# Text attention scored once in 32x32 array tiles, with each partition's own maximum and in-place transposes on VectorE, in three of four batches

## Chip, cores and metric

The kernel runs on one core of one Trainium2 chip. The metric is the device time of one execution in microseconds. Five engines have queues of their own: PE (TensorE, matmuls), DVE (VectorE), ACT (ScalarE), POOL (GpSimd) and SP (here only DMA issues). Each takes its instructions strictly in the order of the program; they meet through semaphores.

## The reference

A layer with cross attention and a quantised feed-forward part, on 4 batches of 1024 tokens with 512 channels. Of the 1024 tokens, 768 are "image" tokens in three chunks of 256, which attend to their own chunk; the last 256 are "text" tokens, which attend to all image tokens and causally to the text tokens. 16 heads of 32 channels.

```python
def trinity_mask(txt_tok, img_tok):
    sit = img_tok // 3
    img_img = (i < img_tok) & (j < img_tok) & (i // sit == j // sit)
    txt_img = (i >= img_tok) & (j < img_tok)
    txt_txt = (i >= img_tok) & (j >= img_tok) & (i >= j)
    return img_img | txt_img | txt_txt

def xattn(q, kv, ...):          # B, N, C = 4, 1024, 512; H = 16; d = 32
    qh, kh, vh = heads(q @ Wq + bq), heads(kv @ Wk + bk), heads(kv @ Wv + bv)
    scores = jnp.einsum('bhqd,bhkd->bhqk', qh, kh) * d ** -0.5
    attn = softmax(where(mask, scores, -inf), axis=-1)
    out = jnp.einsum('bhqk,bhkd->bhqd', attn, vh)
    return out.transpose(0, 2, 1, 3).reshape(B, N, C) @ Wo + bo

x = x + xattn(layernorm(x), ctx, ...)
x = x + ffn(layernorm(x), ...)   # gate, up (512 -> 1408), silu, down; int8-like fake quantisation
```

## The kernel before

The program has an attention stage (to about 874 us of the profiled execution) and a feed-forward stage behind it. All instructions of PE, DVE, ACT and POOL stand in an order that the program writes out by hand (`manual_schedule`, L819).

**Blocks and units.** A block is 256 query tokens of one batch (`Block`, L412). A unit (`Unit`, L424) is one block with one group of four heads (`g`, 128 channels); in a text block also one of four parts of 256 keys, so that a text block has 16 units and an image block 4. The batches come in turn: three image blocks and the text block; in the last batch the text block comes second. There are 112 units.

**The loop over units** (L864) makes one step per unit, and each step works on several units at once: scores of unit n, transposed scores and exponentials of unit n-5 (`T_LAG`), values of unit n-6 (`V_LAG`). Between them stands one "large" piece: a quarter of a key/value projection, a half of a query projection (`big_step`), or half of an output projection (`step_output`); `large` and `target` say which, by a count of work. Each is about 3.4 us of PE.

**Scores are made twice.** `maxima` (L435) makes scores with queries on partitions, four heads in four row groups of the array (32 x 128 tiles, L446 for image, L457 for text), and DVE takes the row maximum (L450, L468; in text the causal mask is added first, L467). POOL splits the negated maximum into two bfloat16 parts (`minus_maxima`, L472), and a DMA transpose brings them into a row (`shifts`, L488). `weights` (L495) makes the scores a second time with keys on partitions (L509), on top of a matmul that lays the shift into the same PSUM tile (L504); ACT takes two exponentials of 1024 columns (L514, L518). POOL adds the weights up over the key tiles (L535). `values` (L539) multiplies the values with the weights in four column groups (128 x 32 tiles, L554), and the sums with ones (L573); ACT copies both out, DVE takes the reciprocal (L588) and POOL the product (L589), which is the normalised output with channels on partitions.

**Projections.** `load_spread` (L142) loads a block of tokens so that one DVE transpose of 32x32 blocks (L267) turns it; its source is read with a step of four elements, since channel 4p + k goes with row p of weight slice k. PSUM: three pairs of two banks for scores (`ps_sc`), one bank for values (`ps_av`), one for projections (`ps_mm`).

**Weights of the feed-forward part** are quantised in the attention stage: per 128 rows a load, a maximum on DVE, a quantisation on ACT and POOL, and a DMA transpose into `wgT` and `wuT`, which stay on chip (`weight_unit`, L645).

Of the kernel before, what the change touches and what calls it, by code (L numbers as in the profile page):

```python
# [42 lines left out]
def kernel(ctx: ExitStack, tc: tile.TileContext, x, kv, Wq, bq, Wk, bk, Wv, bv, Wo, bo, clip_x, clip_down, w_gate, w_up, w_down, out):  # L43
# [39 lines left out]
    wgT = cpool.tile([P, NCC, FF], BF16, tag="wgT", name="wgT")  # L83
    wuT = cpool.tile([P, NCC, FF], BF16, tag="wuT", name="wuT")
# [36 lines left out]

    with ExitStack() as actx:
# [3 lines left out]
        qp = actx.enter_context(tc.tile_pool(name="qp", bufs=4))  # L126
        kp = actx.enter_context(tc.tile_pool(name="kp", bufs=7))
        ap = actx.enter_context(tc.tile_pool(name="ap", bufs=1))
        wp = actx.enter_context(tc.tile_pool(name="wp", bufs=1))
# [12 lines left out]
        def load_spread(src, c):  # L142
            t = ld.tile([P, NQB * 2, P], F32, tag="cb", name=f"spread_{c}")
            s = src.rearrange("(k q) (c m) -> c q k m", q=D, c=NCC)
            for i in range(NCC):
                nc.sync.dma_start(t[i * D : (i + 1) * D], s[i])
            return t

# [13 lines left out]
        for _ in range(14):  # L162
            nc.tensor.matmul(idle.rearrange("p (a b) -> p a b", a=4), onesb, rhs, start=True, stop=True)
        cb0 = load_block(kv_tok, 0, "cb")
        for ci in range(NCC):
            (nc.sync if ci % 2 == 0 else nc.scalar).dma_start(W["Wk"][:, ci, :], Wk.rearrange("(p k) f -> k p f", k=NCC)[ci])
# [4 lines left out]
        for name, w in (("Wv", Wv), ("Wq", Wq)):  # L171
            nc.sync.dma_start(W[name], w.rearrange("(p k) f -> p k f", k=NCC))
# [15 lines left out]
        def output_bias():  # L188

            bvr = wk2.tile([P, NCC, D], F32, tag="wst", name="bvr", bufs=1)  # L190
            parts = wk2.tile([P, C], F32, tag="sp", name="bo_parts")
# [24 lines left out]


        Q, K, V = {}, {}, {}
# [17 lines left out]
        def prepare(a):  # L236

            j = jobs[a]
            if j.kind == "kv":
                spreads[a] = load_spread(kv_tok[j.c * QB : (j.c + 1) * QB, :], f"kv_{j.c}")  # L240
                return
            spreads[a] = load_spread(xn_d[j.c], f"q_{j.c}")
            next_queries(j.c)
# [7 lines left out]
        class Job:  # L251
# [8 lines left out]
            def run_small(self):  # L260
# [4 lines left out]
                if self.c > 0:  # L265
                    src = spreads.pop(self.a)
                    nc.vector.transpose(self.T.rearrange("p c (k q) -> p k c q", q=D), src.rearrange("p k (e c) -> p k c e", c=NCC))  # L267
                    return
# [6 lines left out]
                cols = src[:, i, :].rearrange("p (f k) -> p k f", k=NCC)  # L275
                for cc in range(NCC):
                    nc.tensor.transpose(pt[:, cc, :], cols[:, cc, :], ident)
# [24 lines left out]
            def first_rows(self):  # L302

                K[0] = kp.tile([P, NCC, QB], F32, tag="kT", name="kT_0")
# [14 lines left out]
            def run_big(self, half=False):  # L319
# [8 lines left out]
                elif i < 2:  # L328
                    if i == 0 and first:
                        K[c] = kp.tile([P, NCC, QB], F32, tag="kT", name=f"kT_{c}")  # L330
                    rest = self.rows(K[c], "Wk", NCC, 1.0, 2 * i, parts)
                else:
                    i -= 2
                    if i == 0 and first:
                        V[c] = kp.tile([P, 2, C], F32, tag="va", name=f"va_{c}")
# [16 lines left out]
        background = deque()  # L352
        ready = {}

        def normalise(c):
# [25 lines left out]
            def apply():  # L381
                for i in range(2):
                    nc.scalar.activation(xb[:, i, :], xb[:, i, :], AF.Identity, bias=t[:, i : i + 1], scale=s[:, i : i + 1])
                if c > 0:
                    nc.sync.dma_start(xn_d[c].rearrange("(t p) c -> p t c", p=P), xb)
                ready[c] = True
# [23 lines left out]
        OUTS = 3  # L410
# [13 lines left out]
        class Unit:  # L424
            def __init__(self, block, g, part, parts):
                self.k, self.g, self.part, self.parts = block, g, part, parts
                self.direct = False
                self.n = f"{block.n}_{g}_{part}"
# [6 lines left out]
        def maxima(u):  # L435
# [15 lines left out]
            else:  # L451
# [12 lines left out]
                for h in range(2):  # L464
# [3 lines left out]
                    nc.vector.tensor_reduce(nmh[:, h, :, i, half], s[:, :, :n], AX.X, ALU.max, negate=True)  # L468

# [25 lines left out]
        def weights(u, between):  # L495
# [16 lines left out]
            pT = wk2.tile([P, 4, 2, QB], F32, tag="pT", name=f"pT_{u.n}")  # L512
# [26 lines left out]
        def values(u, between, more=False):  # L539
# [7 lines left out]
            av = state["av"]  # L547
            diag = k.text and u.part == TEXT
# [15 lines left out]
            if last:  # L564
# [19 lines left out]
                avs = small.tile([P, 2, QB], F32, tag="avs", name=f"avs_{u.n}", bufs=2)  # L584
# [58 lines left out]
        quantised = [False]  # L643

        def weight_unit(n):  # L645

            src, dst, scales, what = (w_gate, wgT, sg, "g") if n % 2 == 0 else (w_up, wuT, su, "u")
# [3 lines left out]
            w8 = wk2.tile([P, C], I8, tag="w8", name=f"w8_{what}_{ic}", bufs=1)  # L651
            q = wk2.tile([P, C], BF16, tag="wqt", name=f"wq_{what}_{ic}", bufs=1)
# [9 lines left out]
            def quantise():  # L662
                nc.scalar.activation(w8, w, AF.Identity, scale=rcp)
                nc.gpsimd.tensor_copy(q, w8)
                quantised[0] = True

            def transpose():
                nc.sync.dma_start_transpose(dst[:, :, ic * P : (ic + 1) * P], q)

            return largest, quantise, transpose  # L670

        T_LAG, V_LAG = 5, 6
        units = []
        for b in range(B):
            for qb in range(NQB) if b < B - 1 else (0, TEXT, 1, 2):
                k = Block(b, qb)
                parts = NQB if k.text else 1
                units += [Unit(k, g, part, parts) for g in range(NCC) for part in range(parts)]
        n_img, n_text = NCC * TEXT, NCC * NQB
# [3 lines left out]
        for i, u in enumerate(units):  # L683
            u.direct = u.direct or u.part == TEXT and i + V_LAG >= LATE
        last_of = {c: max(n for n, u in enumerate(units) if c in u.k.keys) for c in range(NC_)}


        then_q = dict(zip(Q_ORDER, Q_ORDER[1:] + [None]))
# [3 lines left out]
        KV_BUFS = 7  # L692
# [3 lines left out]
        def prepare_next(n, force=False):  # L696

            a = at_small
            if a < len(jobs) and a > 1 and a not in prepared:
                j = jobs[a]  # L700
                while force and j.kind == "q" and not ready.get(j.c):
                    background.popleft()()
# [573 lines left out]
```

## Time and profile before

| what | us |
|---|---|
| three runs | 1127.98, 1126.76, 1128.59 (median 1127.98) |
| span of the profiled execution | 1126.9 |
| first scores of a unit start | 30.7 |
| the three text blocks of batches 0, 1, 2 | 128 to 252, 342 to 465, 554 to 676 |
| last output projection of the attention stage starts | 873.7 |
| first matmul of the gate starts, last one | 884.1, 1038.4 |
| mean granted TensorE clock | 0.995 |

Times on the page are microseconds from the span's start unless they are marked ns. A line of a group names the source line, the engine, the operation, the tile written and the tiles read, the shapes and the number; then busy time and mean ns of one; then the idle time of the engine just before them and what ended most of it. A float32 matmul leaves two MATMUL records. Matmuls overlap each other, so the mean ns of one is longer than what each adds to the busy time.

### The profile page before, as it was taken

What the parts mean: (1) busy time and instruction counts of PE and PEld (TensorE: products, weight loads), DVE (VectorE), ACT (ScalarE), POOL (GpSimd) and SP (SyncE); (2) the same over time, 40 slices, a digit from 0 to 9 for tenths busy, and PEclk for the clock granted to TensorE, in tenths of its full rate; (3) what the DMA queues carried; (4) which work ended last, traced back from release to release, by engine and by line L of the source; (5) the groups of instructions that cost most, each with busy time, mean ns of one, the idle gap of its engine ahead of it and who ended that gap; (6) DMA issues with size and microseconds to landing.
All of it is one profiled execution on the core that took longest, in us unless ns stands there. A gap on an engine that the chain in (4) does not pass through costs nothing.

```text
span 1126.9 us, 31493 instructions
## 1 busy us (share of the span) xinstructions
PE 1106.6 (98%) x13829; PEld 553.9 (49%) x13851; DVE 783.9 (70%) x980; ACT 502.4 (45%) x701; POOL 532.0 (47%) x615
## 2 busy tenths in 40 slices
PE   9999999999999999999999999999999899998998
PEld 5545545454545444454545445555554344443344
DVE  2546677666576857666777657777667788877887
ACT  3234434353544334444434345545433465553553
POOL 1224546577755467775446467566752222110110
PEclk9999999999999999999999999999999899999999
DMA  7379645255744444332222113112321599310895
GB/s 234 101 219 284 114 96 127 61 113 98 121 62 115 93 105 78 101 81 63 59 84 80 48 60 83 47 51 63 114 67 58 179 295 255 70 38 23 302 386 194
DMA packets 138257, 135.87 MB, mean 121 GB/s; under 512 B 56060, under 2 KB 103432, under 8 KB 136712
## 3 DMA queue, kind: packets, MB, share of 16 engines
q1 hardware_dynamic: 115600, 91.91, 29.5%
q0 software_dynamic: 22208, 41.42, 14.3%
q8 instruction: 108, 1.77, 0.7%
q10 hardware_dynamic: 312, 0.53, 0.2%
q14 instruction: 29, 0.24, 0.1%
HBM read 79.96 MB, written 50.07 MB: 115 GB/s over the span
## 4 chain that ended last, share of the span: by engine, by line
PE 87%; POOL 4%; DVE 3%; ACT 2%; DMA 2%; issue 1%; SPq 0%; DVEq 0%; POOLq 0%; ACTq 0%
PE pv L226 10%; PE po L226 9%; PE av L554 9%; PE pp_q L226 8%; PE pp_kv L226 8%; PE t L509 7%; PE pg L1116 7%; PE pu L1116 7%; PE s L457 5%; PE pd L1219 5%; PE s L446 4%; POOL sp L535 3%; PE av L573 3%; PE t L504 3%; PE pd L1207 1%
## 5 line engine op out<-in xcount | busy, mean ns | idle before, releaser
L514 ACT ACTIVATE pT<-t 128x1024 f32<-128x1024 f32 x112 | 114.8, 1025 | 330.2 <-PE t L509 299.8
L535 POOL TENSOR_TENSOR sp<-sp,pT 128x1024 f32<-128x1024 f32 x84 | 189.3, 2254 | 43.2 <-ACT pT L518 39.8
L468 DVE TENSOR_REDUCE nmh<-s 128x2 f32<-128x1024 f32 (+1 forms) x128 | 145.2, 1157 | 61.2 <-PE s L457 59.0
L535 POOL TENSOR_TENSOR sp<-pT 128x1024 f32<-128x1024 f32 x59 | 140.2, 2375 | 95.7 <-ACT pT L518 87.3
L450 DVE TENSOR_REDUCE nmh<-s 128x4 f32<-128x1024 f32 x96 | 112.7, 1216 | 85.7 <-PE s L446 85.7
L226 PE MATMUL pp_q<-qT,Wq_sb 128*32 128x256 f32 x2048 | 121.3, 380 | 0.2
L226 PE MATMUL pv<-Wv_sb,kvT 128*32 128x512 f32 (+1 forms) x1088 | 120.5, 570 | 0.0
L554 PE MATMUL av<-pT,va 128*32 128x256 f32 (+1 forms) x1792 | 116.9, 377 | 0.0
L518 ACT ACTIVATE pT<-t 128x1024 f32<-128x1024 f32 x112 | 114.5, 1023 | 0.0
L509 PE MATMUL t<-qT,kT 32*128 32x256 f32 (+1 forms) x1792 | 113.8, 367 | 0.0
L226 PE MATMUL pp_kv<-kvT,Wk_sb 128*32 128x256 f32 x1920 | 112.5, 380 | 0.1
L226 PE MATMUL po<-Wo_sb,oT 128*32 128x512 f32 (+1 forms) x1120 | 112.1, 534 | 0.3
L588 DVE RECIPROCAL avs<-avs 128x256 f32<-128x256 f32 x63 | 109.8, 1743 | 0.0
L589 POOL TENSOR_TENSOR oT<-avs 128x256 f32<-128x256 f32 x63 | 48.0, 762 | 104.2 <-DVE avs L588 104.2
L509 PEld LDWEIGHTS t<-qT,kT 32*128 32x128 f32 x1792 | 88.3, 184 | 6.6
L1116 PE MATMUL pg<-xqT,wgT 128*128 128x512 bf16 x344 | 89.9, 381 | 1.1 <-DVE xqT L1077 0.5
L1116 PE MATMUL pu<-xqT,wuT 128*128 128x512 bf16 x345 | 89.8, 381 | 0.4
L1122 ACT ACTIVATE silu<-pg,sg 128x512 f32<-128x512 f32 x88 | 60.0, 686 | 64.9 <-PE pg L1116 62.8
L226 PEld LDWEIGHTS pp_q<-qT,Wq_sb 128*32 128x32 f32 x2048 | 63.3, 110 | 48.3 <-issue 5.8
L1143 DVE SCALAR_TENSOR_TENSOR h<-pu,su,silu 128x512 f32<-128x512 f32 x88 | 65.3, 746 | 30.3 <-PE pu L1116 27.6
L226 PEld LDWEIGHTS pp_kv<-kvT,Wk_sb 128*32 128x32 f32 x1920 | 60.2, 110 | 43.6 <-issue 2.3
L554 PEld LDWEIGHTS av<-pT,va 128*32 128x32 f32 x1792 | 47.0, 109 | 53.5 <-issue 30.3
(190 smaller groups left out, 1435.0 us busy)
## 6 DMA issues: line engine op xcount, KB each, us to landing
xt<-x_d SPq DMA_DIRECT2D x16, 1024.0 KB, 6.0
h<-h_d POOLq DMA_DIRECT2D x3, 2816.0 KB, 13.5
xb<-in_x_dram SPq DMA_DIRECT2D x16, 512.0 KB, 4.4
x_d<-bo_b SPq DMA_DIRECT2D x16, 512.0 KB, 5.7
x_d<-in_x_dram POOLq DMA_DIRECT2D x16, 512.0 KB, 7.6
xr<-x_d SPq DMA_DIRECT2D x16, 512.0 KB, 3.8
x_d<-xr POOLq DMA_DIRECT2D x16, 512.0 KB, 3.8
spread_kv<-in_ctx_dram SPq DMA_DIRECT2D x60, 128.0 KB, 3.0
```

Source lines behind the costliest of these rows:

```text
L226: nc.tensor.matmul(out[rows_of(j)], lhs[:, rows_of(j)], rhs, start=start, stop=stop, tile_position=(0, j * D), skip_group_check=True)
L450: nc.vector.tensor_reduce(nmh[:, h, :, :, 0], prs[h], AX.X, ALU.max, negate=True)
L468: nc.vector.tensor_reduce(nmh[:, h, :, i, half], s[:, :, :n], AX.X, ALU.max, negate=True)
L509: nc.tensor.matmul(prs[j // 2][:, j % 2, n, cols], kc[rows_of(j), g, n * P : (n + 1) * P], q[rows_of(j), g, cols], start=False, stop=(n == 1))
L514: nc.scalar.activation(pT[:, :2], prs[0], AF.Exp)
L518: nc.scalar.activation(pT[:, 2:], prs[1], AF.Exp)
L535: nc.gpsimd.tensor_tensor(sp[:, :, cols], a, pT[:, :, n, cols], ALU.add)
L554: nc.tensor.matmul(av[rows_of(j), 0, cols], va[:, n, g * P + j * D : g * P + (j + 1) * D], u.pT[:, j, n, cols], start=(u.part == 0 and n = ...
L588: nc.vector.reciprocal(avs[:, 1, :], avs[:, 1, :])
L1116: nc.tensor.matmul(ps, w[:, cc, ic * P : (ic + 1) * P], qT[:, cc, :], start=(cc == 0), stop=(cc == NCC - 1))
L1122: nc.scalar.activation(s, pg, AF.Silu, scale=sg[:, ic : ic + 1])
L1143: nc.vector.scalar_tensor_tensor(h[:, ic, :], pu, su[:, ic : ic + 1], s, ALU.mult, ALU.mult)
```

## The change

In batches 0, 1 and 2 a text unit is now 64 consecutive queries (two blocks of 32) against all the keys they may attend to, for four heads; there are still 16 of them per text block (`u.rows`). The text block of batch 3 and all image blocks keep the old way.

- `block_scores` makes scores once, in 32 matmuls of 32 x 32 array tiles: 4 heads on the row groups, 4 key sets on the column groups, 2 query blocks. A partition then holds one query and a quarter of its keys. DVE adds a mask to the last 16 columns and takes the partition's own maximum (`own`).
- `exponents`: eight exponentials (one per head and query block, 208 to 256 columns, bias is the own maximum), each with a sum of its row (`accum_out`).
- `spread_out`, `exchange`, `differences`, `factors`, `inverses`: the four partitions that hold one query get each other's maxima and sums through a matmul with a 0/1 matrix (`same`), and from them one factor per row.
- `scaled`: POOL multiplies the exponentials in place by the factor, so that they are normalised. `turned`: DVE transposes them in place in 32x32 blocks, after which keys lie on partitions.
- `row_values`: one product with the values for each two units, in four column groups, 28 or 32 matmuls per half block of queries; ACT copies the result straight to `oT`.

Beside it: five empty steps (`GAP`) ahead of each of these text blocks; projections in these blocks are counted 1.2 to 1 (`TEXT_PACE`); keys of a batch in one tile, two of them (`kp`), six value and three query buffers; `pT`, `avs` and the new exponentials share three buffers (`bp`); the contraction order of the projections is changed so that the transposes of L267 read consecutive elements, and weights are loaded in pieces to match; text keys of batches 0 to 2 are loaded with every fourth token together (`turned=True`); the quantised gate and up weights are transposed into a small tile, written to DRAM and loaded back when the projection weights are no longer needed (`reload`); stores and weight transposes are issued one step later (`posts`).

The core of the diff:

```diff
+        def block_scores(u):
+            k, g, q, keys = u.k, u.g, Q[u.k.c], KB[u.k.b]
+            u.s = prs = [pair(f"s_{u.n}_{h}") for h in range(2)]
+            u.own = small.tile([P, 2, 8], F32, tag="own", name=f"own_{u.n}", bufs=3)
+            for a in range(2):
+                block = slice((2 * u.part + a) * D, (2 * u.part + a + 1) * D)
+                for x in range(4):
+                    for j in range(4):
+                        nc.tensor.matmul(
+                            prs[j // 2][x * D : (x + 1) * D, j % 2, a, :].rearrange("p (k n q) -> p k n q", n=2, q=D),
+                            q[rows_of(j), g, block],
+                            keys[rows_of(j), g].rearrange("p k (n g q) -> p g k n q", n=2, q=D)[:, x],
+                            start=True, stop=True, tile_position=(j * D, x * D), skip_group_check=True,
+                        )
+            u.width = 3 * 2 * D + 16 * (u.part + 1)
+            for h in range(2):
+                s, w = prs[h], u.width
+                nc.vector.tensor_tensor(s[:, :, :, w - 16 : w], s[:, :, :, w - 16 : w], mask16..., ALU.add)
+                nc.vector.tensor_reduce(out, s[:, :, :, :w], AX.X, ALU.max, negate=True)
+        def exponents(u, h):
...
+            for x in range(4):
+                y = 4 * h + x
+                nc.scalar.activation(
+                    u.e[:, y // 2, 2 * (u.part % 2) + y % 2, :w], u.s[h][:, x // 2, x % 2, :w], AF.Exp, bias=u.own[:, 0, y : y + 1], accum_out=u.own[:, 1, y : y + 1]
+                )
+        def spread_out(u):
+            nc.gpsimd.tensor_tensor(u.ex, own, group.unsqueeze(2).to_broadcast([P, 4, 16]), ALU.mult)
+        def exchange(u):
+            bank_ = ps_av.tile([P, 2, QB], F32, tag="av", name=f"all_{u.n}")
+            nc.tensor.matmul(bank_[:, 0, :64], same, u.ex.rearrange("p x c -> p (x c)"), start=True, stop=True)
+        def differences(u):
+            nc.vector.tensor_reduce(least, u.all[:, :, 0, :].rearrange("p x y -> p y x"), AX.X, ALU.min)
+            nc.vector.tensor_tensor(u.w[:, :4], least.unsqueeze(1).to_broadcast([P, 4, 8]), u.all[:, :, 0, :], ALU.subtract)
+            nc.vector.tensor_tensor(u.w[:, 4], least, u.own[:, 0, :], ALU.subtract)
+            nc.vector.tensor_copy(u.sums, u.all[:, :, 1, :])
+        def factors(u):
+            nc.gpsimd.tensor_tensor(u.w[:, :4], u.w[:, :4], u.sums, ALU.mult)
+            nc.gpsimd.tensor_tensor(u.w[:, :2], u.w[:, :2], u.w[:, 2:4], ALU.add)
+            nc.gpsimd.tensor_tensor(u.w[:, 0], u.w[:, 0], u.w[:, 1], ALU.add)
+        def inverses(u):
+            nc.vector.reciprocal(u.w[:, 0], u.w[:, 0])
+        def scaled(u):
+            nc.gpsimd.tensor_tensor(u.f, u.w[:, 4], u.w[:, 0], ALU.mult)
...
+            if u.part % 2 == 0:
+                nc.gpsimd.memset(half[:, :, :, u.width : u.width + 16], 0.0)
+            for h in range(2):
+                e = half[:, 2 * h : 2 * h + 2, :, : u.width]
+                nc.gpsimd.tensor_tensor(e, e, f, ALU.mult)
+        def turned(u):
+            w = 7 * D if u.part < 2 else QB
+            for h in range(2):
+                e = u.e[:, 2 * h : 2 * h + 2, 2 * (u.part % 2) : 2 * (u.part % 2) + 2, :w]
+                nc.vector.transpose(e, e)
+        def row_values(u):
+            av = ps_av.tile([P, 2, QB], F32, tag="av", name=f"av_{u.n}")[:, 0, :]
+            half, blocks = u.part // 2, 7 if u.part < 2 else 8
+            for x in range(blocks):
+                for j in range(4):
+                    nc.tensor.matmul(
+                        av[rows_of(j), :P].rearrange("p (a q) -> p a q", q=D),
+                        V[k.keys[x // 2]][:, x % 2, g * P + j * D : g * P + (j + 1) * D],
+                        u.e[:, j, :, x * D : (x + 1) * D],
+                        start=(x == 0), stop=(x == blocks - 1), tile_position=(0, j * D), skip_group_check=True,
+                    )
+            nc.scalar.copy(k.oT[:, g, half * P : (half + 1) * P], av[:, :P])
```

The order of one step in the loop, with `now` the unit of this step, `r1` and `r2` those one and two steps back, and `r` three back (`R_LAG`):

```diff
+            if r is not None and r.part % 2:
+                row_values(r)
...
+                if u.rows and u.k.text:
+                    block_scores(u)
+                else:
+                    maxima(u)
...
+            if r1 is not None:
+                spread_out(r1)
...
+            if now is not None:
+                exponents(now, 0)
             full = large(n)
+            if now is not None or r1 is not None:
+                complete()
+            if r1 is not None:
+                exchange(r1)
+                differences(r1)
+            if now is not None:
+                exponents(now, 1)
+            if r1 is not None:
+                nc.scalar.activation(r1.w, r1.w, AF.Exp)
+                factors(r1)
+            if r2 is not None:
+                turned(r2)
+            if r1 is not None:
+                inverses(r1)
+                scaled(r1)
```

## The prediction

> **What bounds the kernel now.** I read the busy totals first, then the chain of work that ended last, then that chain in order of time in one text block, then the costliest groups, and last a table of busy time by stretch.
>
> ```profile
> PE 1106.6 (98%) x13829; PEld 553.9 (49%) x13851; DVE 783.9 (70%) x980; ACT 502.4 (45%) x701; POOL 532.0 (47%) x615
> ...
> PE 87%; POOL 4%; DVE 3%; ACT 2%; DMA 2%; issue 1%; SPq 0%; DVEq 0%; POOLq 0%; ACTq 0%
> ```
>
> TensorE is busy for 98% of the span and carries 87% of the chain that ended last; no other engine has a twentieth of it. One step (one unit's scores to the next unit's) in a text block, from that chain in order of time; the columns are start, length, engine, tile, line and number of records (a float32 matmul leaves two):
>
> ```profile
> 151.99 3.57 PE po L226 x32
> 155.56 0.33 PE t L504 x4
> 155.88 0.86 PE t L509 x16
> 156.75 1.00 PE av L554 x16
> 157.75 0.43 PE av L573 x8
> 158.18 3.43 PE pv L226 x32
> 161.61 1.08 PE s L457 x16
> ```
>
> The pieces touch: nothing but TensorE sets the pace. The table by stretch says the same for a whole text block of 16 steps, with the other engines at 43 to 70%:
>
> ```profile
> core 0: us, PE busy (x) PEld busy (x) DVE busy (x) ACT busy (x) POOL busy (x), PEclk, DMA share, GB/s
> 128.00:252.00 124.00, 122.75 (x1832) 61.87 (x1832) 86.76 (x108) 52.95 (x80) 76.24 (x74) 1.00 0.44 96
> 342.00:465.00 123.00, 122.55 (x1836) 61.71 (x1832) 88.68 (x112) 51.82 (x77) 72.50 (x67) 1.00 0.45 100
> ```
>
> So a text step takes 123/16 = 7.7 us, and the other engines have 2.3 to 4.4 us of it free. The groups from which the new operations are priced, with mean ns and idle time:
>
> ```profile
> L535 POOL TENSOR_TENSOR sp<-sp,pT 128x1024 f32<-128x1024 f32 x74 | 176.6, 2386 | 42.4 <-ACT pT L518 39.8
> L589 POOL TENSOR_TENSOR oT<-avs 128x256 f32<-128x256 f32 x63 | 48.0, 762 | 104.2 <-DVE avs L588 104.2
> L267 DVE STREAM_TRANSPOSE qT<-spread_q 128x1024 f32<-128x1024 f32 x15 | 32.0, 2132 | 26.3 <-PE pp_q L226 15.9 <-DMA spread_q<-xn_d 8.0 <-PE pv L226 2.3
> L450 DVE TENSOR_REDUCE nmh<-s 128x4 f32<-128x1024 f32 x96 | 112.7, 1216 | 85.7 <-PE s L446 85.7
> L309 PE MATMUL pk<-kvT,Wk_sb 128*128 128x256 f32 x32 | 7.2, 382 | 0.1
> L226 PE MATMUL pp_q<-qT,Wq_sb 128*32 128x256 f32 x2048 | 121.3, 380 | 0.2
> ```
>
> The last two show what array tiles give: the same 256 columns cost 7.2/32 = 225 ns on the whole array and 121.3/2048 = 59 ns in four column groups at once.
>
> **The change on TensorE alone.** Out, for one head group of a text block (four units): scores 1.08, shift product 0.33, transposed scores 0.86, values 1.00, four times each, and the sums 0.43: 13.5 us. In: four times 32 score matmuls, 64 records of 256 columns in 32x32 tiles. No row has sixteen tiles at once. If all sixteen run together they are four waves of 216 ns, 0.86 us; at the 59 ns of four groups they are 3.8 us. I take 0.86, since these tiles are row groups (L509, 16 records in 0.86) crossed with column groups (L226), and each kind alone reaches nearly fourfold. With 0.2 for the change of array shape (1.08 against 0.86 above), 4.2 us. Four exchange matmuls of 64 columns, 0.3 each with its change of shape: 1.2. Values: 60 matmuls with 128 columns, 120 records at half of 1.00/16: 3.7. Sum 9.1, so 4.4 us saved; times 12 groups (three batches), 53 us. If TensorE stayed the bound: 1126.9 - 53 = 1074 us, and 18 us less for a text block: 105 us.
>
> [...]
>
> **The change on the other engines, by step.** ScalarE: eight exponentials with a bias and a sum in place of two of 1024; 256 columns with a bias take 471 ns (L295), two follow each other in 0.84, so 3.4 us, and reading eight sums costs from nothing to 8 x 0.2 (the shortest ScalarE rows, L371). With one projection's eviction (0.9), the exponential of the differences and the copy of the values, 5 to 6.7 us. VectorE: two masks 0.5, two maxima over some 930 columns 2.2, four small operations on 8 to 32 columns 0.7 (L478: 169 ns), a reciprocal 0.2, two transposes. These have no dense row. L267 takes 2.13 us for 1024 but reads with a step of four elements; the new ones read in order, as does L450, 1.2 us. For 960 on average that is 1.1 or 2.0 each. I take 1.1, since the order of reading is what sets L267 apart; 2.0 goes into the range. In all 5.8 or 7.6, and 0.9 of spreading and statistics.
>
> [...]
>
> GpSimd: in place of the running sums (2.39 per 1024, seven in four units) two in-place products over 930 columns. It is the same operation, L535: 2.39 x 930/1024 = 2.17 each, 4.35; spreading 64 elements 0.35 (between L485, 8 elements, 239 ns, and L589), three factors 0.7, one scale and half a memset 0.35. 5.8 us.
>
> Every engine's sum is under 7.7 us. But they are not independent, and this is the step that decides. In the new order GpSimd issues the spreading of unit k+1 behind the products of unit k; TensorE's exchange of k+1 waits for the spreading; VectorE's differences of k+1 wait for the exchange; behind them in VectorE's queue stand the transposes of k, and behind these the reciprocal of k+1; GpSimd's products of k+1 wait for the reciprocal. That is a loop through three engines that is run once for each unit:
>
> - spreading 0.35
> - exchange, VectorE waiting on it, 0.5 (the lone matmul pair L112 keeps VectorE idle 0.6 with 128 columns)
> - differences 0.7
> - transposes of the unit before 2.2 (ScalarE's exponential and GpSimd's factors, 1.1, beside them)
> - reciprocal 0.2, scale and memset 0.35, some 0.15 for hand-overs
> - products 4.35
>
> 8.8 us, against TensorE's 105/16 = 6.6. No projection can be moved into the hole by the hardware, as TensorE takes its instructions in order and the next projection stands behind the exchange. The engines' other work (maxima 2.7 us, exponentials) fits beside the 4.35 of the products. A text block then takes 27 + 15 x 8.8 = 159 us: an estimated 23 until the first unit's products end (two steps of TensorE and one pass of the loop), and 4 for the last unit's transposes and values. That is 54 us more than 105, 162 for three blocks: 1074 + 162 = **1236 us**, and this is the forecast. The loop becomes harmless at 27 + 15 x P = 105 + 18, P = 6.4 us, where the 53 us saved are just used up.
>
> Edits costed at nothing, as TensorE's queue covers them: the projections' transposes now read in order (one micro-second off, or none, thirty times, off the path; the chain shows L267 once); the quantised gate and up weights go to DRAM and come back in two loads, 1.4 MB each (h<-h_d, 2.8 MB, lands in 13.5 us), issued on SP's queue while the last image blocks run; uncovered, they would hold the feed-forward stage up by some 14 us. The stores and transposes of weights wait on SP's queue behind compute once more per piece; the loads behind them have several steps to spare. Weight rows loaded in pieces of 2 KB: bounds -3 to +3 us at the start (Wk lands in 5 to 6 now). The five empty steps ahead of a text block hold their projections and the image units' remains, so their work only moves. Fewer key and query buffers: the order on TensorE already has it.
>
> **Rivals.**
> 1. Transposes stay at 2.0 each. For it: the only row of a transpose. Against: its reading step. The loop is 10.6, a block 186, 1074 + 243 = 1317 us.
> 2. The loop is shorter, not slower than before: GpSimd's product with a repeated factor runs at the pace of one input. L1067 (512 elements, 622 ns) and L1099 (1408, 1362) give 0.83 ns an element, 0.97 each, so P = 6.4, the 27 becomes 25, a block 121 and the time 1122 us; with the hand-overs overlapped, 6.25, 1115. It decides from about 1 us a product. Against: L535 and L589 are this very operation at 2.3 and 3.0 ns an element.
> 3. Sixteen tiles do not run together: 3.8 in place of 0.86 us. In the steps where the loop has room (6.6 + 2.9 against 8.8) it costs 0.7, and in the first three of a block 2.9: 3 x (13 x 0.7 + 3 x 2.9) = 53 more, 1290 us. Against: the two kinds of groups each run together.
> 4. The loop is hidden and TensorE bounds: 1074 us. For it: TensorE is the bound now. Against: the order of the queues.
>
> **Numbers.** The forecast 0.58, rival 1 0.18, rival 3 0.09, rival 2 0.08, rival 4 0.03, others 0.04. The range 1140 to 1335 leaves out rivals 2 and 4, some of rival 1 above it, and the others. The forecast's own range, from products of 2.0 to 2.4 and waits that add up to half a microsecond a step, is 1205 to 1275. This kernel's runs lie within 0.16% of each other, so 0.2% is about what can be told from no change. Faster: most of rival 2, and rival 4, 0.08; within 0.2%: 0.02; slower: 0.90. The profiled execution took 1126.9 us and the median of the runs is 1127.98, so I add 1: 1237.
>
> **What would show it.** In a text block TensorE busy near 70%, idle before the exchange matmul and released by GpSimd; VectorE's idle before the small minimum released by that matmul; GpSimd's idle before the scale released by the reciprocal. A score unit of 0.9 to 1.1 us, a transpose near 1.1, a product near 2.2, steps of 8.8 us. I am wrong if the products take 1 us, if text steps are below 6.5 us, or if the time goes to the feed-forward stage, which should keep its 249 us from the first L112 (878) to the end.

## The result, and the profile after

The changed kernel takes 1371.5 us (median of four runs, 1371.4 to 1371.9) where the kernel before takes 1128.3 beside it: a ratio of 1.216, 95% interval 1.214 to 1.217, so slower by 243 us. The forecast was 1237 us with a range to 1335. The direction was right; the time lies 134 us above the forecast and above the range.

The page of the profiled execution (span 1369.7 us, mean granted clock 0.911 where it had been 0.995) begins with the busy totals; then the slices of the span, and the chain of work that ended last by engine:

```profile
PE 1170.8 (85%) x15915; PEld 592.4 (43%) x15915; DVE 872.2 (64%) x1341; ACT 588.3 (43%) x1434; POOL 549.0 (40%) x845
...
PE   9899977675899877757998877558999989999898
...
PEclk9999998886899988877999888669999999999999
...
PE 70%; DVE 12%; POOL 8%; ACT 5%; issue 3%; DMA 1%; SPq 0%; DVEq 0%; POOLq 0%
```

TensorE is no longer the only engine of the chain, its share of the span falls from 98 to 85%, and in the three places where it is least busy the granted clock falls too. That TensorE's busy time rises from 1106.6 to 1170.8 is the surprise: the forecast had it fall by 53.

The table by stretch, for the first text block (from its first scores to the first image scores), the image units and empty steps after it, and two neighbouring pieces within the block, cut where the clock changes; behind it the image stretch of the kernel before:

```profile
core 0: us, PE busy (x) PEld busy (x) DVE busy (x) ACT busy (x) POOL busy (x), PEclk, DMA share, GB/s
162.40:332.80 170.40, 127.16 (x2396) 67.00 (x2393) 108.74 (x217) 81.67 (x320) 86.12 (x144) 0.84 0.35 79
332.80:448.90 116.10, 104.40 (x1444) 51.26 (x1446) 73.82 (x92) 40.54 (x62) 59.33 (x80) 0.94 0.51 97
286.40:293.20 6.80, 5.35 (x109) 3.79 (x120) 3.11 (x7) 3.18 (x12) 4.12 (x8) 0.50 0.63 81
293.20:306.90 13.70, 9.88 (x227) 5.36 (x196) 11.07 (x25) 6.51 (x28) 7.27 (x16) 1.00 0.19 53
```

```profile
252.00:342.00 90.00, 88.14 (x1296) 43.26 (x1288) 56.61 (x59) 39.13 (x57) 64.61 (x78) 1.00 0.57 94
```

A text block takes 170.4, 167.2 and 165.6 us (159 forecast). Its steps are not even: after the first four they alternate between some 5.5 and 14 to 15 us, some 20.2 for a pair of units. The last two rows of the first table together last about as long as such a pair: 6.8 us at half clock, 13.7 at full.

The trace's clock records hold two values only, 1.0 and 0.5. That allows the loss to be added up, for the time to the gate's first matmul, as a sum over TensorE's records. "Half clock" is half of the time that TensorE was busy while the clock was 0.5. It is an estimate of what the low clock added, since it takes all work to last twice as long there; in this trace eight records of an output projection took 1.93 us at half clock and 1.04 at full, 64 score records 2.38 and 1.49.

| us | before | after | difference | forecast |
|---|---|---|---|---|
| TensorE's work at full clock | 872 | 857 | -15 | -53 |
| added by half clock | 1 | 78 | +76 | no term |
| TensorE idle | 10 | 191 | +180 | +162 |
| gate starts | 884.1 | 1125.8 | +242 | +109 |

After that little differs: 249.7 us from the first L111 to the end, against 248.6 from the first L112 before, as forecast.

Where the time lies is another matter. The three text blocks take 503 us against 369, 134 more (forecast 108). The stretches around them, up to the gate, take 108 more, where the forecast had nothing: 116.1 in place of 90.0 in the rows above, for one. Some work went over: TensorE's work at full clock falls by 57 us within the text blocks, and some 24 us of that (by the number of their records) are projections that now stand outside; outside, work rises by 42. Of the 191 us idle 133 lie within the text blocks and 58 outside, of the 78 by half clock 61 and 17.

The groups whose prices the forecast had to guess (busy, mean ns; idle before them and its releaser), with shapes kept apart:

```profile
L592 POOL TENSOR_TENSOR E<-E,fac 128x1024 f32<-128x1024 f32 x24 | 44.9, 1894 | 0.9
L592 POOL TENSOR_TENSOR E<-E,fac 128x832 f32<-128x832 f32 x24 | 37.3, 1574 | 0.0
L599 DVE STREAM_TRANSPOSE E<-E 128x1024 f32<-128x1024 f32 x48 | 57.0, 1221 | 2.0 <-POOL E L592 1.8
L599 DVE STREAM_TRANSPOSE E<-E 128x896 f32<-128x896 f32 x48 | 50.3, 1085 | 0.0
```

and, where the shape does not matter:

```profile
L546 ACT ACTIVATION_READ_ACCUMULATOR E<-s,own 128x1 f32 x384 | 83.1, 216 | 0.0
L521 PE MATMUL s<-kT,qT 32*32 32x256 f32 x3072 | 81.2, 436 | 2.6 <-ACT E L546 2.6
L608 PE MATMUL av<-E,va 128*32 128x128 f32 x1440 | 96.6, 418 | 65.6 <-DVE E L599 65.6
L559 PE MATMUL all<-ex,same 128*128 128x64 f32 x96 | 23.2, 327 | 74.4 <-POOL ex L554 74.4
```

The transposes cost 1.1 to 1.2 us, as forecast; the products 1.6 to 1.9, less than the 2.17 forecast. The small score tiles, 81.2 us busy for 3072 records, are 26 ns each (64 records: 1.7 us, or 1.49 where the clock was full; forecast 0.86 and 0.2), and the values products 67 ns (forecast 31). TensorE waits in the two places that are new in its queue: for the spreading (L554) ahead of the exchange, and for the transposes (L599) ahead of the values product. So far this looks like the forecast's loop. The chain in order of time (start, length, engine, tile, line, records) shows another; one pair of steps:

```profile
248.98 3.20 PE av L608 x52
252.18 1.48 PE s L521 x60
253.66 3.64 PE pp_kv L260 x64
...
257.32 0.84 ACT kT L330 x2
258.16 1.67 ACT E L546 x8
259.83 0.13 ACT wall L1120
...
260.03 0.26 POOL wall L574
...
260.90 0.21 DVE wall L580
...
261.46 3.75 POOL E L592 x2
265.21 0.26 POOL ex L554
...
265.52 0.45 PE all L559 x2
...
265.99 0.20 DVE least L567
...
266.58 0.31 DVE E L599
...
267.66 1.21 DVE E L599
...
268.91 3.63 PE av L608 x60
```

From one values product to the next, 19.9 us, the chain passes through four engines' queues in turn: values product, next scores, a projection; then ScalarE, which must evict that projection and finish the unit's exponentials before it comes to the exponential of the differences; factors, reciprocal, one pair of GpSimd products; spreading, exchange, differences, transposes; and the values product again. It is run once for two units. The forecast's loop, with the measured prices, would be 0.27 + 0.5 + 0.6 + 2.1 + 0.2 + 0.35 + 0.15 + 3.5 = 7.7 us a unit, shorter than the 10.1 that a unit takes.

### The profile page after: what moved, and what is told of

Its sections match the earlier page's. It is cut to its first block, busy times and chain, and to the rows that moved or that the text cites. A ratio compares the mean times of both kernels' runs of the same rounds, so it can differ in the third digit from the quotient of the medians.

```text
span 1369.7 us, 37140 instructions
## 1 busy us (share of the span) xinstructions
PE 1170.8 (85%) x15915; PEld 592.4 (43%) x15915; DVE 872.2 (64%) x1341; ACT 588.3 (43%) x1434; POOL 549.0 (40%) x845
## 4 chain that ended last, share of the span: by engine, by line
PE 70%; DVE 12%; POOL 8%; ACT 5%; issue 3%; DMA 1%; SPq 0%; DVEq 0%; POOLq 0%
PE pv L260 7%; PE po L260 7%; PE pp_q L260 7%; PE av L608 6%; PE pp_kv L260 6%; PE pg L1352 6%; PE pu L1352 6%; POOL E L592 5%; PE av L708 4%; PE pd L1455 4%; DVE E L599 4%; PE t L660 4%; PE s L488 3%; PE s L521 3%; ACT E L546 3%
## 5 line engine op out<-in xcount | busy, mean ns | idle before, releaser
L546 ACT ACTIVATE E<-s,own 128x208 f32<-128x208 f32 (+3 forms) x384 | 169.6, 465 | 154.0 <-DVE own L535 138.4
L592 POOL TENSOR_TENSOR E<-E,fac 128x832 f32<-128x832 f32 (+3 forms) x96 | 164.4, 1734 | 1.9
L687 POOL TENSOR_TENSOR sp<-pT 128x1024 f32<-128x1024 f32 x47 | 111.7, 2376 | 119.1 <-ACT pT L670 92.0
L608 PE MATMUL av<-E,va 128*32 128x128 f32 x1440 | 96.6, 418 | 65.6 <-DVE E L599 65.6
L666 ACT ACTIVATE pT<-t 128x1024 f32<-128x1024 f32 x64 | 65.6, 1024 | 169.3 <-PE t L660 162.8
L535 DVE TENSOR_REDUCE own<-s 128x4 f32<-128x832 f32 (+3 forms) x96 | 108.0, 1125 | 3.3
L599 DVE STREAM_TRANSPOSE E<-E 128x896 f32<-128x896 f32 (+1 forms) x96 | 107.3, 1153 | 2.0 <-POOL E L592 1.8
L608 PEld LDWEIGHTS av<-E,va 128*32 128x32 f32 x1440 | 70.5, 169 | 86.7 <-issue 60.3
L742 DVE RECIPROCAL pT<-pT 128x256 f32<-128x256 f32 x51 | 88.9, 1743 | 20.3 <-ACT pT L1182 20.3
L559 PE MATMUL all<-ex,same 128*128 128x64 f32 x96 | 23.2, 327 | 74.4 <-POOL ex L554 74.4
L521 PE MATMUL s<-kT,qT 32*32 32x256 f32 x3072 | 81.2, 436 | 2.6 <-ACT E L546 2.6
```

The lines of the kernel that those rows point to most:

```text
L521: nc.tensor.matmul(prs[j // 2][x * D : (x + 1) * D, j % 2, a, :].rearrange("p (k n q) -> p k n q", n=2, q=D), q[rows_of(j), g, block], key ...
L535: nc.vector.tensor_reduce(out, s[:, :, :, :w], AX.X, ALU.max, negate=True)
L546: nc.scalar.activation(u.e[:, y // 2, 2 * (u.part % 2) + y % 2, :w], u.s[h][:, x // 2, x % 2, :w], AF.Exp, bias=u.own[:, 0, y : y + 1], ac ...
L592: nc.gpsimd.tensor_tensor(e, e, f, ALU.mult)
L599: nc.vector.transpose(e, e)
L608: nc.tensor.matmul(av[rows_of(j), :P].rearrange("p (a q) -> p a q", q=D), V[k.keys[x // 2]][:, x % 2, g * P + j * D : g * P + (j + 1) * D] ...
```

## The experiments

Twelve kernels, each timed in one round against the kernel before; intervals are given with the ratios. Theory G is the forecast's loop, theory A the loop of the chain above, T that TensorE itself is the bound, K that the halved clock is a cause and not only a symptom.

**late**: the values product goes from the front of its step to its end.

```diff
-            if r is not None and r.part % 2:
...
-                row_values(r)
...
             if r1 is not None:
                 inverses(r1)
                 scaled(r1)
+            if r is not None and r.part % 2:
...
+                row_values(r)
```

> The values product (row_values) is moved from the front of its step to its end, behind the exchange. Theory A (a loop over two units: values product 3.6, scores 1.5, projection 3.6, its eviction 0.8 and the exponentials 1.7 on ScalarE, then factors, GpSimd products, exchange, differences, transposes 2.0, and again the values product, 20.3 us a pair): the loop falls apart, what is left is the forecast's loop with measured prices, 7.6 us a unit, so a text block goes from 167 to some 130 us and the whole to 1240 to 1290 us. Theory G (the forecast's loop through spreading, exchange, transposes, reciprocal and products already sets the pace and the values product waits beside it): no more than 10 us less, 1360 us. Theory T (TensorE's lower clock and slow small tiles set the pace): within 15 us of 1371.

Measured 1311.3 us, 1.164 (1.161 to 1.167): 60 us less. Theory T falls, and G too, since its loop was not touched. But A expected 80 to 130.

**early**: only the forecast's edge, spreading behind products, is cut.

```diff
-            if r1 is not None:
-                spread_out(r1)
...
+            if now is not None:
+                spread_out(now)
             if r1 is not None:
                 inverses(r1)
                 scaled(r1)
```

> Only the spreading is moved: that of unit n is issued ahead of the products of unit n-1 on GpSimd, so that the exchange no longer waits for them. Theory A: one of the two products in the loop of a pair drops out, 20.3 to some 17 us a pair, 24 pairs, some 70 to 80 us less: 1290 to 1310 us. Theory G: this is the edge that closes the loop, steps of 6.6 to 7 us, 1190 to 1220 us. Theory T: within 15 us of 1371.

Measured 1344.2 us, 1.193 (1.190 to 1.197): 27 us less. That is far from G, and less than A expected. Read again after the result, A's expectation was misread from the chain: the loop passes the products once for a pair, not twice, and the cut takes out only the spreading, exchange and differences between products and transposes, some 1.4 us, 24 times: 34.

**late_early**: both moves.

> Both moves together. Theory A: both loops are open; left are TensorE's own 6.6 us a unit and the chain products, transposes, reciprocal, products at 6.1 us, so text blocks of 110 to 120 us and 1130 to 1200 us, at a granted clock back above 0.96. Theory G: as the spreading alone, 1190 to 1220. Theory T: above 1340, the clock near 0.91.

Measured 1290.5 us, 1.146 (1.142 to 1.149): 81 us less, nearly the sum of the two, and 90 above the top of A's range. A is right in its direction, but behind its loop stands something nearly as long. Three lines of this kernel's waits (what waited for what, us in total, times, longest) name it:

```profile
POOL wall L574 <- ACT wall L1109: 135.5, 42, 9.1
ACT E L546 <- DVE own L535: 121.0, 41, 11.2
...
DVE wall L580 <- POOL wall L576: 47.2, 43, 2.7
```

GpSimd waits for ScalarE's exponential of the differences, ScalarE for VectorE's maxima, and VectorE, at the reciprocal, for GpSimd: a ring, closed because the next unit's maxima stand behind the reciprocal in VectorE's queue. Theory C below.

**noprod**: the products touch 16 columns in place of 832 to 1024 (the normalisation of the rest is left out).

```diff
-                nc.gpsimd.tensor_tensor(e, e, f, ALU.mult)
+                nc.gpsimd.tensor_tensor(e[:, :, :, :16], e[:, :, :, :16], f[:, :, :, :16], ALU.mult)
```

> The two in-place products of GpSimd touch 16 columns in place of 832 to 1024, so most rows are left without their normalisation; everything else stays. Theory A: 7 us of the 20.3 of a pair go, and a pair is then bound by what is left of the loop and by TensorE, 13 to 14 us: 1371 - 24 x 6.5 = 1215, between 1190 and 1240. Theory G: the same or more, down to 6.6 us a unit, 1190. If GpSimd's products lie off the path: above 1340.

Measured 1339.1 us, 1.189 (1.185 to 1.192): 32 us less, 99 above A's range and at the edge of the case that the products lie off the path (above 1340). The largest term of the forecast's loop, and a piece of A's, taken away almost whole, is worth 32 us. With 24 pairs that is 1.3 us of the 3.75 that the chain showed for a pair. The waiting moved: TensorE's wait for the exchange falls from 74.4 to 21.7 us, its wait for the transposes rises from 65.6 to 98.0:

```profile
PE av L608 <- DVE E L599: 98.0, 48, 5.5
PE all L559 <- POOL ex L554: 21.7, 7, 3.4
```

**le_norecip**: late_early without the reciprocal (the sum itself is multiplied).

> The version with both moves, and the reciprocal on VectorE is left out (the sum is multiplied in place of its inverse, so the rows are normalised wrongly). Theory C (a third loop, by the order of VectorE's queue: the next unit's maxima stand behind the reciprocal, which waits for GpSimd's factors, these for ScalarE's exponential of the differences, this for the eight exponentials, these for the maxima: 1.3 + 1.9 + 0.85 + 1.9 + 0.3 + 0.9 + 0.2, 7.3 us a unit and more in steps with a values product): nothing on VectorE waits for the factors any more, and steps go from 8.1 to near 7: 1290 - 48 x 1.1, some 1225 to 1255 us. Theory D (the transposes, which wait for the products of the unit before, hold VectorE up, or TensorE's scores wait for the score tiles to be read): under 10 us less, 1280 to 1290.

Measured 1267.4 us, 1.124 (1.121 to 1.127): 23 us less than late_early. C expected 35 to 65, D at most 10. It lies between them: the ring has a part, and again not alone. The reciprocals that are left out also took 10 us of VectorE themselves (48 of 0.21), so the ring's own part is not separated.

**deep**: no operation is added or removed, but everything from the exponential of the differences on comes one step later, and stands ahead of the new unit's work on ScalarE.

```diff
+            if r2 is not None:
+                nc.scalar.activation(r2.w, r2.w, AF.Exp)
             if now is not None:
                 exponents(now, 0)
...
-            if r1 is not None:
-                nc.scalar.activation(r1.w, r1.w, AF.Exp)
-                factors(r1)
             if r2 is not None:
-                turned(r2)
-            if r1 is not None:
-                inverses(r1)
-                scaled(r1)
+                factors(r2)
+                inverses(r2)
+                scaled(r2)
+            if r3 is not None:
+                turned(r3)
+            if r is not None and r.part % 2:
+                row_values(r)
```

> The values product at the end of its step, and everything from the exponential of the differences on (factors, reciprocal, scale and products, transposes) one step later, the exponential ahead of the next eight exponentials on ScalarE, the reciprocal ahead of the transposes on VectorE, the values product one more step later; buffers for it. No operation is added or taken away. If order alone made the loss (theories A and C), no loop under TensorE's own work is left: 6.8 to 7.2 us a step, text blocks of 115 to 125 us, 1140 to 1180 us in all, clock above 0.96. If the small tiles, the lowered clock or ScalarE's sums (8 exponentials with reads, 3.8 us, an eviction 0.9, the rest) set the pace: 1230 or more.

Measured 1266.6 us, 1.123 (1.120 to 1.126): 105 us less than the change as it is. The expectation that no loop would be left fails: the time falls on the other side, above 1230. That does not yet refute order as the cause, since the new order has waits of its own, above all GpSimd's products for the reciprocal:

```profile
POOL fac L585 <- DVE wall L580: 88.0, 48, 4.9
```

**deep2**: deep, with the factors, the scale and the products first on GpSimd, the reciprocal right behind the maxima, and the values product behind the scores again.

> The version one step deeper, once more reordered: ahead of all other work of the step GpSimd gets the spreading, the factors, the scale and the products, VectorE the reciprocal right behind the maxima, and the values product stands behind the scores again, now with its transposes a step old. What remains of the loops in the deeper version is, by its trace, GpSimd's products waiting 88 us for the reciprocal, which stands in VectorE behind the differences, which wait for the exchange, which waits for the spreading behind the products, and the values product waiting 32 us for the bank that the exchange holds. Theory (order alone): both go, 6.8 to 7.3 us a step, 1195 to 1235 us, clock above 0.96. Rival (VectorE's 6.3 us a step with its background work is the bound, or the score tiles are): above 1250.

Measured 1261.6 us, 1.119 (1.113 to 1.124), not told apart from deep. The theory of order alone had at most 1235; the time lies in the rival's range, above 1250. It is the best order found. Its waits on TensorE, and a text block with the image units that follow it:

```profile
PE s L521 <- ACT E L546: 30.0, 20, 3.4
PE all L559 <- POOL ex L554: 15.9, 8, 4.6
PE s L488 <- DVE nmh L492: 15.5, 4, 4.5
```

```profile
419.60:543.20 123.60, 111.56 (x2306) 59.44 (x2302) 100.12 (x197) 77.34 (x307) 73.65 (x135) 0.94 0.32 85
543.20:665.40 122.20, 108.37 (x1492) 54.59 (x1490) 80.72 (x107) 44.17 (x77) 57.00 (x76) 0.93 0.27 73
```

The exchange's wait is down from 74 to 16 us and this text block from 167 to 124, which is nearly the time of the same block before (123); the first one takes 132, from 170. But the stretch after it holds five empty steps with projections and takes 122 in place of 89, so a batch takes 246 against 212. TensorE's sum for it is 867 at full clock, 44 by half clock and 102 idle: what is left against the kernel before is 92 us of waiting and 43 by half clock. The largest wait is that of the scores for the exponentials that still hold their score tiles, 30 us, the second half of the rival; this was not taken further.

**fill** and **fill2**: dummy matmuls in TensorE's holes, so that the clock stays up.

```diff
+            for _ in range(16 if u.part % 2 == 0 else 0):
+                nc.tensor.matmul(bank_[:, 1, :]..., onesb, onesb..., start=True, stop=True)
             nc.tensor.matmul(bank_[:, 0, :64], same, ...)
...
+            for _ in range(16):
+                nc.tensor.matmul(av[:, 1, :]..., onesb, onesb..., start=True, stop=True)
```

(fill has the first sixteen in every unit.)

> Sixteen small bfloat16 matmuls of 256 columns, whose result nobody reads, are put ahead of each exchange and each values product of the changed kernel, 1.7 us of TensorE work where it waits 3 to 6 us. Theory K (the clock is halved after TensorE has been idle for a while: 235 us at half clock before the gate, in which 156 us of work cost 78 us more, and the values products after a wait are the work that is hit, 66 ns a record against 31): the granted clock goes above 0.96, the values products to 35 to 45 ns a record, and 24 pairs get 1 to 2 us shorter, 1320 to 1350 us in spite of the added work. If the clock only follows the waits and costs nothing: 1365 to 1400 us.

> The small matmuls that nobody reads are put only where TensorE waits in the changed kernel: sixteen ahead of each values product and sixteen ahead of the exchanges of the first unit of each pair. Filling every exchange had taken the long step from 14.8 to 12.7 us and the short one from 5.4 to 7.0. Theory K (half clock lies on the path, through the values product): 5.4 and 12.7, 18.1 in place of 20.2 us a pair, 24 pairs, 50 us: 1310 to 1335 us, clock above 0.96. If the lower clock has no part in the time: 1360 to 1375.

Measured 1358.8 us, 1.205 (1.200 to 1.210), and 1343.8, 1.191 (1.185 to 1.198): 13 and 28 us less, with 129 and 89 us of useless work added at full clock. Both miss their expectation by some 9 us above the range, but less time with more work is what K says and its rival excludes (for fill2, 1360 to 1375). Records of the values product, changed kernel first, then fill (ns, least/median/most):

```profile
L608 PE MATMUL av<-E,va x1440: 272/421/423, 207.9 to 914.5; 128*32 128x128 f32 x180
```

```profile
L613 PE MATMUL av<-E,va x1440: 272/273/423, 213.2 to 901.1; 128*32 128x128 f32 x180
```

The median goes from the half-clock to the full-clock duration (421 to 273 ns), the values products from 67 to 39 ns a record (35 to 45 expected), and the mean clock from 0.911 to 0.974 (fill2: 0.964).

**split**: each score matmul cut in two of 128 columns.

> Each score matmul of the row units is cut into two of 128 columns, the same scores and outputs. If 24 ns between two starts is a floor that the number of columns doesn't move, a unit's scores leave 128 records at 24 to 25 ns and take 3.1 us in place of 1.5, and the whole gets 35 to 75 us longer (once or twice a pair in the loop), 1405 to 1445. If the time goes with the columns: 12 to 13 ns a record and 1371 to 1380 us.

Measured 1396.1 us, 1.238 (1.234 to 1.242), and

```profile
L522 PE MATMUL s<-kT,qT 32*32 32x128 f32 x6144 | 138.9, 285 | 4.3 <-ACT E L547 2.5 <-issue 1.7
```

138.9/6144 is 22.6 ns a record with half the columns, where 256 columns had 26 (81.2/3072; 23 in the units at full clock). In these two runs the time goes with the number of records, not with the columns. That it is a floor between two starts is not shown: in the changed kernel's trace the first 32 records of a unit start mostly 6 to 7 ns apart, in two groups of sixteen that follow each other in 240 ns; then come some 0.3 us with a single start, and the rest start mostly 16 to 17 ns apart. What sets the pace was not tried (each record has a weight load of its own, 3072 here, and split doubles these too, 6144). The time rose by 25 us, less than expected: more than half of the added 58 us of TensorE work, by this difference, fell into its waits.

**rowsoff** and **pace**: the change without its row units and empty steps.

```diff
-                rows = k.text and b < B - 1
+                rows = False
```

(rowsoff with 5 query and 7 value buffers and smaller weight buffers; pace also with TEXT_PACE 1.0.)

> The rest of the change without its row units: no text block goes by rows and there are no empty steps; the text blocks of batches 0 to 2 are computed as before (their keys stay in the new order of loading, so that the mask falls on other keys), with 5 query, 7 value and smaller weight buffers. Theory: the loss is the row units' alone, and the weights by way of DRAM, the pieces of weight rows, the later stores and the new contraction order cost nothing: 1124 to 1134 us. Rival (they cost a part of the 243): above 1145.

> The rest of the change without its row units once more, with the text blocks' projections counted 1.0 to 1 as before (TEXT_PACE 1.0). If the 33 us that the rest costs come from the places that the changed count gives to the projections: 1130 to 1145 us. If they come from the other edits (stores and loads issued later, buffers, weights by way of DRAM): 1155 to 1165.

Measured 1161.1 us, 1.030 (1.027 to 1.033), and 1155.4, 1.024 (1.021 to 1.027). Edits costed at nothing cost 27 to 33 us in these two forms; the pace of the projections is 6 of it. By the trace of rowsoff TensorE's work is 5 us more, half clock adds 6 more, and it idles 20 us more, in many waits of at most 2.4 us (for evictions, sums, maxima). Which edit puts them there was not tried, and the buffers differ from the change's, so this is a size and not a cause.

## Why the prediction was right or wrong

The gate starts 133 us later than forecast. By the table this is 76 us of half clock, for which the forecast had no term, 38 us of TensorE work that was not saved, and 18 us more of idle time. By place it is 26 us in the text blocks and 108 around them.

- **That the change makes the kernel slower because TensorE, in order, waits on work that goes through GpSimd, VectorE and back**: right. The longest waits stand ahead of the exchange, released by GpSimd, where the forecast put them, and ahead of the values product. TensorE's idle time, 180 us more, is close to the 162 forecast, but in part by luck: only 131 of it lie in the text blocks, to which the forecast gave all 162.
- **The loop of 8.8 us that "decides"**: wrong in which loop it is. Its terms hold or are shorter (transposes 1.1 as forecast, exchange 0.45, products 1.6 to 1.9 for 2.17), so it would be 7.7; cutting it gave 27 us, taking its products away 32. The step that failed here is "The engines' other work (maxima 2.7 us, exponentials) fits beside the 4.35 of the products": ScalarE's exponentials do not lie beside the loop, since the exponential of the differences stands behind them in its queue, and the values product and a projection stand ahead of the scores that they need. With the values product moved behind the exchange the time fell by 60 us. That the idle time came out nearly right is a coincidence of a loop too long in its products with one that was not seen.
- **"4.4 us saved; times 12 groups, 53 us" on TensorE**: wrong in size, 15 at full clock. The scores were taken at sixteen tiles at once, 0.86 us and 0.2 for the change of shape; a unit took 1.49, which makes 21 us in 48 units. An exchange took 0.45 in place of 0.3, 7 us, and rowsoff shows 5 us that belong to the rest of the change. Starts in the changed kernel come mostly 6 to 7 ns apart within two groups of sixteen, and 16 to 17 ns apart in most of the rest of a unit; a unit at full clock has 23 ns a record, where the 0.86 us had 13. In the kernel before, four records start 6 to 7 ns apart, then a pause of 89 ns follows (L554 with 128 columns), 27 ns a record on average. The values product at 31 ns a record was not shown at full clock: fill, where most of these records have the full-clock duration, took 39, the changed kernel 67, and 73 where the clock was half throughout (56 records in 4.1 us).
- **No term for the clock**: the largest miss, 76 us. The forecast counted on holes in TensorE and priced TensorE's work behind them as if it ran at full clock; nearly every values product of the changed kernel ran at half clock (the mean clock over each of the 24 is 0.50 to 0.56). fill2 halves this term (to 37 us) and is 28 us faster in spite of its added work, so at least that much lies on the path.
- **"Edits costed at nothing"**: 27 to 33 us in the two forms that were run. Among them stood that the work of the five empty steps "only moves": the stretches outside the text blocks grew by 108 us, 42 of it TensorE work that came over, 16 half clock and 50 waiting. How much of the waiting is due to the empty steps was not tried.
- **Rival 1** (transposes at 2.0) fell by the trace, although the time landed nearest to it; **rival 2** fell (products at 1.6 to 1.9, not 1); **rival 3** fell: a unit's scores took 1.49 us, not 3.8, and in the first half of a unit sixteen tiles do run together (240 ns for a group of sixteen, 216 assumed); **rival 4** fell with TensorE's 191 us idle.
- **The feed-forward stage keeps its 249 us**: right, 249.7.

Of the 243 us, then: some 30 by the rest of the change (with other buffers), some 110 given back by order alone (deep2, part of it by the higher clock that came with it), and of the rest the clock and the remaining waits are the parts that can be named. How they divide is open, as filling the holes and reordering were not tried together; and no version beat the kernel before.

## What to carry to other kernels

When work that one engine did alone is spread over several in-order queues, write out for every engine what stands ahead of each instruction in its queue, and follow every ring that closes, not the first that explains a number: here there were at least three, of some 10, 7.7 and 7.3 us a unit by the sums above, and cutting one of them gave only a part of what it cost. What helped most was one more step between the parts of a unit, with buffers for it (deep, 105 us); the score tiles were what it still lacked. Whoever forecasts holes in TensorE of the size seen here should price what runs after them at half clock: in the changed kernel's trace each of 2.0 us and more had half clock within the 4 us behind it.

## What the runs showed of the hardware

In the traces of the kernel before and of the changed kernel the clock changes only at multiples of 3.41 us from its first record (5 and 65 changes). Sorted by TensorE's busy share in each such stretch of the changed kernel's trace: every one at full clock with 50% or less was followed by half clock, every one with 63% or more by full clock; from half clock it came back after stretches with 86% or more, and not after 79%. The kernel before came back to full clock after a stretch with 78%, and kept full clock after one with 52%. So the share goes far, but does not decide alone. A hole shorter than such a stretch was enough: at 265.9 us the clock was halved after a stretch with one hole of 2.9 us, and the like happened once in nearly every pair (of the 32 changes to half clock before the last, 25 came behind holes of 3.3 us at most). Why it changes was not tried beyond fill and fill2.

An exponential that also sums its row leaves a second instruction of 216 ns on ScalarE (L546, 384 of them), 83 us in all. A GpSimd product in which one operand is repeated along the row takes 1.85 to 1.89 ns an element (L592, 1894 ns for 1024 and 1574 for 832), against 2.32 for the sums with two full operands (L687, 2376 ns for 1024).
